# Graph network layer 3 on one core: a second DMA queue for the row sums, and two moves in the order of a period

## The chip, the cores and the metric

The kernel runs on one core of one Trainium2 chip. The metric is device time in microseconds of one execution; the time of a version is the median of several executions. The engines are TensorE (PE, with its weight loads shown apart as PEld), VectorE (DVE), ScalarE (ACT), GpSimd (POOL) and SyncE (SP), whose only work here is to issue DMAs. Each engine takes its instructions in the order in which they were written for it, and semaphores hold an instruction back until what it needs is there. A DMA that an engine issues is one of the instructions in that engine's order; the transfer itself then runs on the core's 16 DMA engines.

## What is computed

The input x has 32 samples of 512 nodes with 64 features, and adj is a 512 x 512 normalised adjacency with few entries. Four layers follow one another, each with a layer norm and a ReLU in front and x added behind. The first three (a graph convolution, a two-step propagation and a one-head attention) take the first 440 us or so and are not touched. The fourth, "layer 3", is this:

```python
def gat_layer(x, graph, W, b):
    h = x @ W
    s = jnp.einsum('bnd,bmd->bnm', h, h) * graph
    s = jnp.where(s == 0.0, NEG_INF, s)
    a = jax.nn.softmax(s, axis=2)
    return jnp.einsum('bnm,bmd->bnd', a, h) + b
heads = jax.vmap(lambda W, b: gat_layer(flow_x, graph, W, b))(Wh, bh)   # 8 heads, 128 wide
...
x = jax.nn.leaky_relu(cat, negative_slope=0.01)
out = gat_layer(x, graph, W_out, b_out)
return jax.nn.leaky_relu(out, negative_slope=0.01)
```

All of it is in float32.

## The kernel before

Layer 3 works in units of two 512 x 512 attention maps. A `Heads` unit holds two heads of one sample (32 samples x 4 = 128 units), an `Out` unit the last attention of two samples (16 units), so there are 144. The two maps lie side by side: the tiles called `p_att` are 128 rows x 2 maps x 512 columns, and a unit has four of them (r = 0 to 3). A unit passes through these steps, whose names are those of the code:

- `scores(r)` (L367, PE) writes logits to a PSUM tile of the pool `ps_s`, which has two buffers; `maxima(r)` (L379, DVE) adds the mask, keeps the negated logits in `p_att` and takes each row's extreme value into `top`.
- `spread_out` and `spread_in` (L384 to L398): DVE turns `top`, SP writes it to DRAM in four small DMAs (L389) and reads it back to all partitions in one of 512 KB (L395, tile `topb`).
- `shift(r)` (L401, POOL) subtracts `topb`; `exps(r)` (L410, ACT) takes the exponential, for r = 1 and 3 into a PSUM tile `e_ps` that shares the two buffers of `ps_s`; `join(r)` (L413, DVE) adds the pair's two exponentials.
- `totals` (L431, PE) sums the columns of the two joined tiles with a matrix of ones, and ACT copies the result to `tot` (L436). `totals_out` (L443) spreads the 4 x 512 sums over 128 partitions, eight to each, with two SP DMAs of 4 KB, one for each half e, into the tile `parts`.
- `recips` (L449, L452, DVE) adds the halves and takes the reciprocal; `recips_out` (L456, SP) writes it to DRAM; `recips_in` (L463, SP, two DMAs of 128 KB), in the next period, brings it back as `recb`.
- `values(j)` (L419, PE) multiplies with the features into one PSUM tile `av` (one buffer); `normalize` (L469, DVE), again in the next period, multiplies `av` by `recb` into `o_att` and so frees `av`.
- Heads units go on with `y_pe` (L551, PE), `y_act` (L561, ACT) and `y_dve` (L569, DVE), which leave the activated head in `cat`. `product(i)` (L597, PE, eight matmul instructions) is one quarter of the multiplication by W_out for two samples; it runs in 64 of the periods. Out units go on with `back` (L641), `back_dve`, `back_pool` (L655) and `store` (L662, SP, two DMAs of 128 KB in 256-byte runs).

The order is written out by hand, for all five engines, in `period(t)` inside `planned` (L708 to L762). Each period works on several units at once: `unit(n)` is the unit that began n periods ago. Since each engine keeps the order of that list, the place of a call fixes its place in the queue of every engine that it uses. Three stretches matter here. On SP a period issues: `recb` x2, `top_row` x4, `topb`, the two output stores if there are any, `parts` x2, `rec_row`. On PE: `scores` 2 and 3, `y_pe`, `scores` 0 and 1 of the unit ahead, `totals`, `values`, `product` if there is one, and then some small preparation (`make_v`, `make_hx`, `make_g`) before the next period's `scores(2)`. On DVE: `maxima` 2 and 3, `y_dve`, `normalize`, `maxima` 0 and 1 of the unit ahead, `join(1)`, `recips`, `join(3)`. On ACT the copy to `tot` is followed at once by `exps(1)` and `exps(3)`.

The first period that does nothing but layer 3 starts at about 463 us; a period takes 10.3 to 14 us.

Of the kernel before, what the change touches and what calls it, by code (L numbers as in the profile page):

```python
# [22 lines left out]
def fast_form(  # L23
# [25 lines left out]
    nc = tc.nc  # L49
    B, N, F = x.shape  # L50
    C = N // P
# [264 lines left out]
    class Pair:  # L316
# [121 lines left out]
        def totals_out(self):  # L438

            self.parts = tiny.tile([P, 2, 8], F32, name="parts")  # L440
            rows = self.tot.rearrange("(k e r) n -> k e r n", k=2, e=2)
            for e in range(2):
                nc.sync.dma_start(  # L443
                    self.parts[:, e], rows[:, e, 0].rearrange("k (g i) -> k g i", i=8)
                )

# [219 lines left out]
    def any_zero():  # L666

        def across(src, rows, name):
            ps = ps_m.tile([P, P], F32, name=name, tag="m")
            n = src.shape[0]  # L670
            nc.tensor.transpose(ps[:rows, :n], src, ident[:n, :n])
            return ps[:rows, :n]

        own = tiny.tile([P, 1], F32, name="own")
        nc.vector.tensor_reduce(own, least, AX.X, OP.min)
        two = tiny.tile([1, 2], F32, name="two")
        nc.vector.tensor_reduce(two[:, 0:1], across(own, 1, "own_ps"), AX.X, OP.min)
        best = tiny.tile([B // 2, 2], F32, name="best")
        nc.vector.tensor_reduce(
            best,  # L680
            across(least_out, B // 2, "out_ps").rearrange("b (k f) -> b k f", k=2),
            AX.X, OP.max,
        )
        worst = tiny.tile([B // 2, 1], F32, name="worst")
        nc.vector.tensor_reduce(worst, best, AX.X, OP.min)
        nc.vector.tensor_reduce(
            two[:, 1:2], across(worst, 1, "worst_ps"), AX.X, OP.min
        )
        flag = tiny.tile([1, 1], F32, name="flag")
        nc.vector.tensor_reduce(flag, two, AX.X, OP.min)  # L690
        nc.vector.scalar_tensor_tensor(
            again, flag, 0.0, unsound, op0=OP.is_equal, op1=OP.max
        )
# [6 lines left out]
    def planned(units, products):  # L700

        class Nothing:
            def __getattr__(self, name):
                return lambda *args: None

        nothing = Nothing()

        def period(t):  # L708
            def unit(lag):
                return units[t - lag] if 0 <= t - lag < len(units) else nothing  # L710

            now, ahead = unit(0), unit(-1)
            for r in range(2, C):
                now.scores(r)
            unit(3).recips_in()
            unit(4).y_pe()
            unit(1).shift(0)
            unit(1).exps(0)
            unit(4).y_act()
            u, i = products.get(t - 1, (None, 0))  # L720
            if u and i == H // 2 - 1:
                u.keep_product()
            unit(1).shift(2)
            unit(1).exps(2)
            for r in range(2, C):
                now.maxima(r)
            now.spread_out()
            now.spread_in()
            for r in range(2):
                ahead.scores(r)  # L730
            unit(4).y_dve()
            unit(3).normalize()
            for r in range(2):
                ahead.maxima(r)
            unit(-3).features(3)
            unit(4).back()
            unit(5).back_pool()
            unit(-2).make_gs()
            unit(5).store()
            unit(2).totals()  # L740
            unit(2).totals_out()
            unit(1).shift(1)
            unit(1).exps(1)
            for j in range(C):
                unit(2).values(j)
            u, i = products.get(t, (None, 0))
            if u:
                u.product(i)
            unit(1).join(1)
            unit(1).shift(3)  # L750
            unit(1).exps(3)
            unit(2).recips()
            unit(2).recips_out()
            unit(4).back_dve()
            unit(1).join(3)
            unit(1).make_v()
            unit(-3).make_hx()
            unit(-2).make_g()
            for step in range(3):
                unit(step - 6).features(step)  # L760
            if t == len(units):
                any_zero()  # L762

        return period
# [1065 lines left out]
```

## Time and profile before

| | us |
|---|---|
| median of 3 runs (lowest, highest) | 2160.28 (2159.49, 2162.55) |
| profiled execution, its own time | 2158.13 |
| its span on the core | 2156.3 |
| PE busy over the span | 2004.3 |
| DVE busy over the span | 1787.3 |
| POOL busy over the span | 1430.5 |
| ACT busy over the span | 1224.3 |

The span is the time from the first to the last profiled instruction of the program; the rest of an execution's time (1.8 us in the profiled one) lies around it. A wait in the profile is the idle time of an engine in front of an instruction, put down to whatever released it last. "Busy" of PE is modelled and says little about how near PE is to its limit; the waits and the chain of waits, which is followed back from the last instruction, say more. Names in the profile have an output, an arrow and inputs: `parts<-tot` is the DMA of `totals_out`.

### The profile page before, as it was taken

The numbers are of one execution on the slowest core, as the hardware profiler recorded it, in microseconds if no ns is written. First come the engines' busy times: TensorE is split into PE (matmuls) and PEld (weight loads), VectorE is DVE, ScalarE is ACT, GpSimd is POOL, SyncE is SP. The second block draws the span as 40 slices with busy tenths as digits, with TensorE's granted clock in tenths as the row PEclk, the third lists the DMA queues.
The fourth block names the chain that finished last, engine by engine and source line by source line (L and its number), as shares of the span: only waits on it lengthen the run. The fifth ranks groups of instructions, "written<-read, shape, count | busy, mean of one in ns | idle before, by whom it ended". The sixth has DMA issues, their size and how long they took to land.

```text
span 2156.3 us, 32793 instructions
## 1 busy us (share of the span) xinstructions
PE 2004.3 (93%) x11038; PEld 836.9 (39%) x11038; DVE 1787.3 (83%) x4257; ACT 1224.3 (57%) x1944; POOL 1430.5 (66%) x697
## 2 busy tenths in 40 slices
PE   7999999979989999999999999999999999999895
PEld 4676776733333333333333333333333333333231
DVE  6799997668888888888888888888889888897984
ACT  3444433336565666565656666656666666665553
POOL 2000000038788888888887888888888887887895
PEclk9999999989999999999999999999999999999998
DMA  5000000002222222222222222222222222222222
GB/s 136 1 1 2 1 1 1 1 21 76 70 65 77 74 70 75 76 65 75 75 71 71 71 71 78 66 76 69 77 71 75 65 76 71 75 66 70 75 66 76
DMA packets 135777, 129.32 MB, mean 60 GB/s; under 512 B 92792, under 2 KB 98080, under 8 KB 135472
## 3 DMA queue, kind: packets, MB, share of 16 engines
q1 hardware_dynamic: 135088, 126.94, 19.9%
q8 instruction: 89, 1.46, 0.3%
q14 instruction: 88, 0.72, 0.1%
q0 software_dynamic: 512, 0.20, 0.1%
HBM read 119.48 MB, written 5.37 MB: 58 GB/s over the span
## 4 chain that ended last, share of the span: by engine, by line
PE 50%; DVE 21%; DMA 11%; POOL 6%; ACT 5%; issue 3%; SPq 3%; POOLq 0%; DVEq 0%; ACTq 0%
PE av L419 14%; DVE p_att L379 11%; PE nt_ps L876 7%; PE s_ps L367 7%; PE acc L968 6%; POOL p_att L401 5%; DMA parts<-tot 4%; PE gT_ps L597 4%; PE g_ps L533 3%; DVE cat L569 3%; DVE p_att L413 3%; DMA topb<-top_row 2%; PE tot_ps L431 2%; DMA recb<-rec_row 2%; DVE o_att L469 2%
## 5 line engine op out<-in xcount | busy, mean ns | idle before, releaser
L401 POOL TENSOR_TENSOR p_att<-p_att,topb 128x1024 f32<-128x1024 f32 x576 | 1346.1, 2369 | 285.0 <-DMA topb<-top_row 148.9
L379 DVE CUSTOM_DVE_ANT_0 p_att<-s_ps,flow_neg 128x512 f32<-128x512 f32 x1152 | 728.6, 685 | 94.4 <-PE s_ps L367 93.2
L367 PE MATMUL s_ps<-hx,g 64*128 64x512 f32 x2048 | 542.2, 618 | 62.8 <-DVE p_att L413 50.1
L410 ACT ACTIVATE e_ps<-p_att 128x1024 f32<-128x1024 f32 x288 | 295.4, 1028 | 187.6 <-DVE top L379 89.8
L410 ACT ACTIVATE p_att<-p_att 128x1024 f32<-128x1024 f32 x288 | 304.2, 1056 | 140.1 <-POOL p_att L401 139.0
L413 DVE TENSOR_TENSOR p_att<-e_ps,p_att 128x1024 f32<-128x1024 f32 x288 | 346.4, 1203 | 35.9 <-ACT e_ps L410 35.2
L367 PEld LDWEIGHTS s_ps<-hx,g 64*128 64x128 f32 x2048 | 176.3, 186 | 371.7 <-DVE top L379 141.8
L419 PE MATMUL av<-p_att,hd 128*64 128x512 f32 x1024 | 272.7, 602 | 28.8 <-DVE o_att L469 24.8
L419 PE MATMUL av<-p_att,hn 128*64 128x512 f32 x1024 | 269.3, 592 | 0.0
L1044 POOL TENSOR_TENSOR x<-x,bias_b 128x512 f32<-128x512 f32 x16 | 20.3, 1272 | 280.5 <-DVE hn L818 280.5
L561 ACT ACTIVATE cat<-y_ps,bh 128x512 f32<-128x512 f32 x256 | 161.0, 680 | 48.0 <-PE y_ps L551 47.0
L569 DVE SCALAR_TENSOR_TENSOR cat<-y_ps,bh,cat 128x512 f32<-128x512 f32 x256 | 178.4, 738 | 11.3 <-ACT cat L561 8.5
L431 PE MATMUL tot_ps<-p_att,ones 128*32 128x512 f32 x1152 | 154.3, 608 | 3.0 <-DVE cat L569 2.5
L419 PEld LDWEIGHTS av<-p_att,hd 128*64 128x64 f32 x1024 | 71.3, 136 | 208.0 <-issue 96.8
L551 PE MATMUL y_ps<-o_att,wh_sb 64*128 64x512 f32 x512 | 142.4, 604 | 0.0
L545 ACT COPY g<-g_ps 128x512 f32<-128x512 f32 x128 | 69.6, 588 | 124.0 <-PE g_ps L533 124.0
L419 PEld LDWEIGHTS av<-p_att,hn 128*64 128x64 f32 x1024 | 85.8, 137 | 133.9 <-issue 133.9
L436 ACT COPY tot<-tot_ps 128x512 f32<-128x512 f32 x144 | 84.3, 585 | 85.1 <-ACT p_att L410 45.6
L968 PE MATMUL acc<-v,s 64*128 64x65 f32 x2048 | 124.0, 280 | 0.7 <-DVE s L954 0.4
L968 PEld LDWEIGHTS acc<-v,s 64*128 64x128 f32 x2048 | 121.1, 195 | 5.9 <-DVE o L984 1.2
L597 PE MATMUL gT_ps<-cat,wo_sb 128*64 128x512 f32 x512 | 122.2, 592 | 0.0
L876 PE MATMUL nt_ps<-adj_t,hn 128*128 128x512 f32 x256 | 117.0, 600 | 0.8 <-DVE hn L840 0.8
(181 smaller groups left out, 2014.9 us busy)
## 6 DMA issues: line engine op xcount, KB each, us to landing
topb<-top_row SPq DMA_DIRECT2D x144, 512.0 KB
recb<-rec_row SPq DMA_DIRECT2D x288, 128.0 KB
top_row<-top_t SPq DMA_DIRECT2D x576, 1.0 KB
parts<-tot SPq DMA_DIRECT2D x288, 4.0 KB
out_dram<-y SPq DMA_DIRECT2D x32, 128.0 KB
x<-in_x_dram SPq DMA_DIRECT2D x3, 1024.0 KB
rec_row<-rec_flow SPq DMA_DIRECT2D x144, 4.0 KB
x<-in_x_dram SPq DMA_DIRECT2D x4, 256.0 KB
```

What stands on the lines that cost most here:

```text
L367: nc.tensor.matmul(ps[:, k], lhsT=g[halves(k), r * P : (r + 1) * P], rhs=x[halves(k), :], start=True, stop=True,)
L379: nc.vector.tensor_tensor_reduce(out=self.p[r][:, k], in0=ps[:, k], in1=flow_neg[:, r], scale=-1.0, scalar=BIG, op0=OP.add, op1=OP.min, ac ...
L401: nc.gpsimd.tensor_tensor(self.p[r], self.p[r], self.topb, OP.subtract)
L410: nc.scalar.activation(to, self.p[r], AF.Exp, scale=-1.0)
L413: nc.vector.tensor_tensor(self.p[r], self.joined, self.p[r - 1], OP.add)
L419: nc.tensor.matmul(self.av[halves(k), :], lhsT=self.v(k, j) if j % 2 else self.less_next(k, j), rhs=self.p[j][:, k], start=(j == 0), stop= ...
L431: nc.tensor.matmul(ps[q : q + 32, :], lhsT=ones, rhs=self.p[2 * e + 1][:, k], start=True, stop=True,)
L561: nc.scalar.activation(self.cat[:, k], self.y[k], AF.Identity, bias=bh01[:, h : h + 1], scale=0.01)
L569: nc.vector.scalar_tensor_tensor(self.cat[:, k], self.y[k], bh[:, h : h + 1], self.cat[:, k], op0=OP.add, op1=OP.max,)
L597: nc.tensor.matmul(self.gps[halves(k), :], lhsT=wo_sb[:, h, :], rhs=Heads.cat.pop((self.b + k, h)), start=(h == 0), stop=(h == H - 1),)
L876: nc.tensor.matmul(p, lhsT=lhs(k), rhs=adj_t[:, k, :], start=(k == 0), stop=(k == C - 1))
L968: nc.tensor.matmul(self.acc[k][:, r], lhsT=self.s[b // 2][halves(k), b % 2, r * P : (r + 1) * P], rhs=self.v[halves(k), b], start=(b == 0) ...
```

## The change

Three edits in layer 3, nothing else. The DMA of the second half (e = 1) of `totals_out` is issued by ACT instead of SP. `unit(5).store()` moves from before `totals` to after `recips_out`. `product(i)` moves from after `values` to before it.

```diff
             self.parts = tiny.tile([P, 2, 8], F32, name="parts")
             rows = self.tot.rearrange("(k e r) n -> k e r n", k=2, e=2)
-            for e in range(2):
-                nc.sync.dma_start(
+            for e, queue in enumerate((nc.sync, nc.scalar)):
+                queue.dma_start(
                     self.parts[:, e], rows[:, e, 0].rearrange("k (g i) -> k g i", i=8)
                 )
...
             unit(-2).make_gs()
-            unit(5).store()
             unit(2).totals()
             unit(2).totals_out()
             unit(1).shift(1)
             unit(1).exps(1)
-            for j in range(C):
-                unit(2).values(j)
             u, i = products.get(t, (None, 0))
             if u:
                 u.product(i)
+            for j in range(C):
+                unit(2).values(j)
             unit(1).join(1)
             unit(1).shift(3)
             unit(1).exps(3)
             unit(2).recips()
             unit(2).recips_out()
+            unit(5).store()
             unit(4).back_dve()
```

On SP a period then issues `recb` x2, `top_row` x4, `topb`, one `parts`, `rec_row`, and the stores if there are any. On ACT the copy to `tot` is followed by the other `parts` DMA, and then by `exps(1)` and `exps(3)`. DVE and POOL keep their order.

## The prediction

> **What bounds the kernel now.** I read the page first (who is busy, and the chain that ended last), then the waits of layer 3 alone (480 to 2110 us), then the instruction timeline of one ordinary period on three engines.
>
> ```profile
> PE 2004.3 (93%) x11038; PEld 836.9 (39%) x11038; DVE 1787.3 (83%) x4257; ACT 1224.3 (57%) x1944; POOL 1430.5 (66%) x697
> ...
> PE 50%; DVE 21%; DMA 11%; POOL 6%; ACT 5%; issue 3%; SPq 3%; POOLq 0%; DVEq 0%; ACTq 0%
> ```
>
> No engine is the bound by itself. PE holds half the chain, DVE a fifth, and transfers a tenth, of which the page gives the transfer `parts<-tot`, the subject of the first edit, 4% of the span: 94 us in 37 pieces by my count along that chain. Now the waits:
>
> ```profile
> DVE p_att L379 <- PE s_ps L367: 92.0, 80, 2.7
> DVE rec_flow L449 <- DMA parts<-tot: 85.6, 105, 2.6
> PE s_ps L367 <- DVE p_att L413: 44.9, 58, 2.1
> PE av L419 <- DVE o_att L469: 24.8, 74, 1.6
> PEld av L419 <- DVE o_att L469: 21.3, 20, 1.9
> ```
>
> (Total us, times, longest.) PE and DVE wait for each other by turns. I sorted these waits by whether the period has a W_out step (64 periods, mean 11.9 us) or not (the rest, mean 11.3 us). With a step PE is the bound: DVE stands 66.5 us in 56 of the 64 before its next `maxima`, for PE's scores, so that its 52 us of waiting for `parts` there cost next to nothing. Without a step DVE is the bound more often: it waits 34 us for `parts` (mean 0.45 us over the 77 such periods that have a `join` behind it), and PE stands 43 us for `join`. The last two rows are the start of `values`, which needs `av` freed by `normalize`; in idle PE time they are 11.6 us in 52 of the step periods and 19.0 us in 62 of the others.
>
> Now one period without a step (start, duration, engine):
>
> ```profile
> 1746.16 0.58 ACT L436 COPY tot<-tot_ps 128x512 f32<-128x512 f32 x1 [0.58 <-ACT p_att L410]
> 1747.46 1.03 ACT L410 ACTIVATE e_ps<-p_att 128x1024 f32<-128x1024 f32 x1 [0.71 <-DVE top L379]
> 1749.10 1.03 ACT L410 ACTIVATE e_ps<-p_att 128x1024 f32<-128x1024 f32 x1 [0.61 <-POOL p_att L401]
> ```
> ```profile
> 1746.33 0.35 SPq L395 DMA_DIRECT2D topb<-top_row  x1
> 1746.77 1.15 SPq L443 DMA_DIRECT2D parts<-tot  x2
> 1750.57 0.34 SPq L456 DMA_DIRECT2D rec_row<-rec_flow  x1
> ```
> ```profile
> 1748.52 1.23 DVE L413 TENSOR_TENSOR p_att<-e_ps,p_att 128x1024 f32<-128x1024 f32 x1
> 1750.13 0.17 DVE L449 TENSOR_REDUCE rec_flow<-parts 128x8 f32<-128x16 f32 x1 [0.39 <-DMA parts<-tot]
> 1750.34 0.20 DVE L452 RECIPROCAL rec_flow<-rec_flow 128x8 f32<-128x8 f32 x1
> 1750.46 1.17 DVE L413 TENSOR_TENSOR p_att<-e_ps,p_att 128x1024 f32<-128x1024 f32 x1
> ```
>
> Three things are to be seen. The SP issues `topb` and both `parts` without a pause, two times 0.57 us for the latter. After the copy to `tot` ends at 1746.74, ACT stands 0.71 us for DVE's `maxima(0)`, which must free a PSUM buffer before the exponential may write `e_ps`: this is the room for a DMA issue on ACT. And the `parts` wait of 0.39 us is followed by a `join(3)` whose exponential had ended at 1750.13, 0.33 us before it began: even with `parts` there at once, DVE would gain no more than that 0.33.
>
> **What the Trainium skill says.** "DMA: Bandwidth & Descriptors", section "Issuing engines are not separate DMA queues", says that issuing from several engines saves only sequencer time, since the transfers run on the same 16 engines. Its section "Queues, rings and completion order" says that SP and ACT each own a ring on each of those engines, and that an engine turns between rings packet by packet. "Why a DMA increments its semaphore by 16 and not by 1" says that a transfer whose slowest dimension is 2 on one side uses two engines; a `parts` DMA reads from two rows (k). The trace agrees where it can: at 1006 us `topb` is issued at 1006.40 and the two `parts` at 1006.80 and 1007.42; the first 64 pairs of 32-byte packets run from 1008.97 to 1009.35, the second follow at once, to 1009.73. Two completion marks end each batch. The first batch thus begins 2.2 us after its issue, where the small `top_row` DMAs need 0.76, directly behind the 4 KB packets of `topb` on its two engines. So the second issue is not what `parts` waits for: the queue behind `topb` is. "Perfetto Trace Analysis", section "DMA Instruction — HWDGE (DVE, Sync)", says that one descriptor generator is shared and locked while in use; no run so far shows two engines issuing at once.
>
> **The change, part by part.** Sums are against the profiled execution, 2158.13 us (span 2156.3 plus 1.8 around it), which lies 2.15 us under the median.
>
> *W_out steps in front of values.* Nothing is added: the same eight instructions, 1.72 us in the chain, stand before `values` instead of behind. They need `cat`, whose second half DVE writes 0.7 us after the first, while `totals`, which starts after the first half, takes 1.04 us; so I expect no new wait. Meanwhile `normalize` ends, 0.2 us or so after `totals`. The 11.6 us of idle in step periods go. `values` ends where the product ended before; its `av` is read some 4 us later. In 56 of 64 such periods PE leads and the gain passes to DVE: 11.6 x 0.87 = 10 us. Bounds: 5 (half is eaten at the next wait) and 11.6.
>
> *A `parts` DMA on ACT.* Removed: one issue of 0.57 us on SP, plus 0.05 between. Gain in landing: 0.62 us where SP is the limit; where the ring is, both batches of 0.38 us still pass the same two engines, and only what ACT's batch can slip in between `topb`'s packets is won, 0 to 0.38 us. If the issues exclude each other, even less. In no-step periods, where DVE goes on without a pause into the next `maxima`, and with the 0.33-like cap in each, my count along the trace gives 4.9 us for a landing 0.2 us earlier, 8.1 us for 0.375 and 11.6 us for 0.6; in step periods 1.2, 2.2 and 3.6. I take 3 us in all, for some 0.1 us, and keep 0 and 15 for the range.
>
> *The same issue on ACT.* ACT's time for it is not in the trace. Nearest row: SP's 0.57 us, begun 0.11 us after the copy ends (1006.69 to 1006.80), so the exponential could start 0.7 us after the copy; were SP's own issue to hold the generator first, about 1.3 us. Today it starts 0.84 us after it in the mean over 143 periods, median 0.75, under 0.7 in 67. Behind it on ACT stand `exps(1)`, `exps(3)` and copies; DVE's `join(1)` waits for the first, PE's next scores for `join`. But `join(1)` is followed by the `parts` wait, 0.45 us, and, as measured to the next `maxima`, another 0.35 us of slack (26.7 us over 77 periods). So a hold of h us costs about 77 x (h - 0.84 - 0.45 - 0.35) = 77 x (h - 1.64): nothing at 0.7 or 1.3 in the mean. For the spread of single periods I charge 1 us; bounds 0 and 27 (h = 2.0). The ACT issue also waits for the earlier `recb` transfer that shares its semaphore; `exps(1)` already waits for that through `normalize`.
>
> *Stores later.* In 16 periods two issues of 0.6 us and the 256-byte packets leave the way of `parts`; nearly all have a W_out step, where a `parts` wait is free. They go to SP between `rec_row` (0.34 us) and `recb`, which waits 1.5 us for `rec_row` to land: 1.3 us of issue fits in. Their packets delay `recb` by up to 1 us, but `rec_row` leaves 1.4 us earlier in those periods. Zero, bounds -3 and +8 (0.5 x 16).
>
> Sum: -10 - 3 + 1 + 0 = -12, 2146 profiled, 2148 as a median.
>
> **The rivals.**
> - *The landing really comes 0.6 us sooner.* For: SP's `parts` issues are 20 us of the chain (39 pieces). Against: the queue behind `topb`. -11.6 - 15 + 1 = -26: 2134. Chance 0.13.
> - *No change.* The PE time freed in step periods reappears as waiting for POOL, which is busy 1363 of 1630 us and has its own loop from `maxima` over `topb` (6 us), four shifts (9.35 us), exponential and `join` back to `maxima`, near two periods; ACT's hold eats the rest. For: POOL's shifts are 5% of the chain. Against: POOL itself waits 147 us for `topb`. -3: 2157. Chance 0.17.
> - *Slower: ACT is held.* A DMA on ACT with its waits keeps the exponentials 2.0 us behind the copy instead of 0.84, in every period: 77 x 0.36 = +27, less 10 from the product: 2177. It decides from h = 1.64 + 10/77 = 1.8 us. For: a third of the periods have under 0.65 us of room. Against: SP does the same issue in 0.57. Chance 0.18.
>
> **How the numbers follow.** Forecast 0.52, the others 0.13, 0.17, 0.18. This kernel's runs tell 0.2%, 4.3 us, from no change. Faster by that: 0.13, 0.47 of the forecast (the rest gains too little) and 0.02 of the third: 0.62. Within: 0.05 of the forecast, 0.13 of the third and 0.02 of the last: 0.20. Slower: 0.16 of the last and 0.02 of the third: 0.18. The forecast's own range is 2141 to 2156 (-19 to -4). Over all cases I leave out the slow half of the last one and the extreme of the first: 2136 to 2165.
>
> **What would show it.** Right: PE's wait for `normalize` at `values` drops to about 19 us plus weight loads' share, with none in periods with a step; DVE's wait for `parts` shrinks by a tenth of a microsecond or so in ordinary periods and vanishes in those with stores; ACT's issue lasts about 0.6 us; and `join` waits for `e_ps` (23.2 us now) grow little. Wrong: a `join` wait of 0.5 us per period, an ACT issue over 1.2 us, or a PE wait in front of the W_out steps. A `parts` wait below half of today's 85.6 us would mean the larger gain.

## The result, and the profile after

The changed kernel takes 2143.76 us in the median of five runs (2141.73 to 2145.79), the kernel before 2159.49 us beside it (2154.81 to 2162.55). The ratio is 0.9931, with a 95% interval of 0.9915 to 0.9946: 14.9 us faster (11.7 to 18.4). Its profiled execution took 2145.48 us, 12.65 less than the one of before.

The page of the kernel after, busy shares and the chain by engine and by line:

```profile
PE 1998.9 (93%) x11038; PEld 819.4 (38%) x11038; DVE 1788.2 (83%) x4257; ACT 1225.9 (57%) x1944; POOL 1431.3 (67%) x697
...
PE 48%; DVE 17%; DMA 13%; POOL 11%; issue 4%; ACT 4%; SPq 2%; POOLq 0%; ACTq 0%; DVEq 0%
POOL p_att L401 10%; PE av L419 10%; DVE p_att L379 9%; PE s_ps L367 8%; PE nt_ps L876 7%; DMA parts<-tot 6%; PE acc L968 6%; PE gT_ps L597 4%; DMA topb<-top_row 4%; DVE p_att L413 4%; PE tot_ps L431 3%; PE g_ps L533 2%; DMA top_row<-top_t 2%; SPq L389 2%; ACT e_ps L410 1%
```

The busy times of PE, DVE, ACT and POOL are within 0.3% of those of before, as they must be: nothing was taken out. The transfer `parts<-tot` has not left the chain; it has 6% now and had 4%. So the chain gives no sign that the gain comes from a shorter transfer. POOL's shifts went from 5% to 10%: in this execution the chain runs over `topb` and POOL more often.

The waits of layer 3, 480 to 2110 us, in the kernel after (total us, times, longest):

```profile
DVE p_att L379 <- PE s_ps L367: 87.3, 82, 2.1
DVE rec_flow L449 <- DMA parts<-tot: 64.2, 100, 2.1
PE s_ps L367 <- DVE p_att L413: 54.8, 61, 8.9
DVE p_att L413 <- ACT e_ps L410: 40.9, 53, 2.9
PE av L419 <- DVE o_att L469: 14.2, 42, 1.9
PEld av L419 <- DVE o_att L469: 14.1, 11, 2.8
```

Two of these answer to the edits. PE's wait for `normalize` at `values`, 24.8 and 21.3 us before, is down to 14.2 and 14.1. Sorted by period, the 11.6 us of PE idle in the 64 periods with a W_out step are gone altogether; 17.1 us stay in the others (19.0 before). And DVE waits 21.4 us less for `parts` (85.6 before), but 17.7 us more for the exponential in front of `join`. Its row in the kernel before:

```profile
DVE p_att L413 <- ACT e_ps L410: 23.2, 39, 1.2
```

Together these two are 108.8 us before and 105.1 after: DVE waits there almost as long as before. In part one wait stands in for the other, as the experiments will show. In part the stores have left the way: in the ten or eleven periods of this stretch that have them, the wait for `parts` fell from 16.1 to 4.5 us.

The third row, PE's wait for `join`, only looks longer than before (44.9 us). Every kernel has one such wait of some 8.9 us at the start of layer 3, at 476.68 us before and 478.88 us after, and only the later one reaches into the stretch that begins at 480 us. Without it 45.9 us are left.

### The profile page after: what moved, and what is told of

Read it like the earlier page. It is cut to its first block, busy times and chain, and to the rows that moved or that the text cites. A ratio compares the mean times of both kernels' runs of the same rounds, so it can differ in the third digit from the quotient of the medians.

```text
span 2143.7 us, 32958 instructions
## 1 busy us (share of the span) xinstructions
PE 1998.9 (93%) x11038; PEld 819.4 (38%) x11038; DVE 1788.2 (83%) x4257; ACT 1225.9 (57%) x1944; POOL 1431.3 (67%) x697
## 4 chain that ended last, share of the span: by engine, by line
PE 48%; DVE 17%; DMA 13%; POOL 11%; issue 4%; ACT 4%; SPq 2%; POOLq 0%; ACTq 0%; DVEq 0%
POOL p_att L401 10%; PE av L419 10%; DVE p_att L379 9%; PE s_ps L367 8%; PE nt_ps L876 7%; DMA parts<-tot 6%; PE acc L968 6%; PE gT_ps L597 4%; DMA topb<-top_row 4%; DVE p_att L413 4%; PE tot_ps L431 3%; PE g_ps L533 2%; DMA top_row<-top_t 2%; SPq L389 2%; ACT e_ps L410 1%
## 5 line engine op out<-in xcount | busy, mean ns | idle before, releaser
L569 DVE SCALAR_TENSOR_TENSOR cat<-y_ps,bh,cat 128x512 f32<-128x512 f32 x256 | 178.3, 738 | 12.8 <-ACT cat L561 10.5
L419 PEld LDWEIGHTS av<-p_att,hn 128*64 128x64 f32 x1024 | 80.0, 137 | 139.8 <-issue 139.8
```

The costliest lines, as they stand in the source:

```text
L419: nc.tensor.matmul(self.av[halves(k), :], lhsT=self.v(k, j) if j % 2 else self.less_next(k, j), rhs=self.p[j][:, k], start=(j == 0), stop= ...
L569: nc.vector.scalar_tensor_tensor(self.cat[:, k], self.y[k], bh[:, h : h + 1], self.cat[:, k], op0=OP.add, op1=OP.max,)
```

## The experiments

All ratios are to the kernel before, run on the same chip beside each of them, with 95% intervals. 2157 us is taken as the time of before where a ratio is turned into microseconds.

**One edit at a time.** Theory A: the moved W_out steps carry the gain. Theory B: the second DMA queue does. Theory C: the stores do. The first three kernels make one edit of the change each, and the fourth makes all but the ACT edit.

```diff
# moved steps alone
-            for j in range(C):
-                unit(2).values(j)
             u, i = products.get(t, (None, 0))
             if u:
                 u.product(i)
+            for j in range(C):
+                unit(2).values(j)
```

> The W_out steps in front of values alone. Theory A (the moved steps carry the gain): the PE idle at the start of values in the 64 periods with a step, 11.6 us, goes to zero and the time falls by 10 to 13 us, ratio 0.994 to 0.9955. Theory B (the second DMA queue carries it): less than half of the 15 us, ratio above 0.9965. Theory C (the stores carry it): the same, above 0.9965.

Measured: 0.9941 (0.9927 to 0.9954), -12.7 us. No PE idle is left at `values` in step periods. Counted from `totals` to the next `totals`, a period with a step takes 11.77 us in the mean instead of 12.00, one without a step 11.15 instead of 11.17: the gain lies where the edit acts. The row of the wait, 24.8 us in the kernel before:

```profile
PE av L419 <- DVE o_att L469: 15.7, 45, 1.7
```

```diff
# ACT edit alone
-            for e in range(2):
-                nc.sync.dma_start(
+            for e, queue in enumerate((nc.sync, nc.scalar)):
+                queue.dma_start(
```

> One parts DMA on ACT alone. Theory A: the ring behind topb sets the landing, so the last parts packet stays at 3.4 us after the issue of topb and the time moves by less than 3 us, ratio 0.9985 to 1.0015. Theory B (the second queue carries the gain): -6 us or more, ratio under 0.997, and DVE's wait for parts falls by 0.3 us a period, 40 us in all. A hold of ACT that costs more than it brings would give a ratio above 1.002.

Measured: 0.9992 (0.9981 to 1.0004), -1.7 us, not to be told from nothing. The last `parts` packet passes 3.39 us after the issue of `topb` (median over the periods, from the packets of the trace); in the kernel before it was 3.41.

```diff
# stores alone
-            unit(5).store()
             unit(2).totals()
...
             unit(2).recips_out()
+            unit(5).store()
```

> The stores after rec_row alone. Theory A: the parts wait shrinks by about 1 us in each of some 9 periods with stores and a W_out step, where DVE would wait for PE anyway: time within 2 us, ratio 0.999 to 1.001. Theory C (the stores carry the gain): -5 us or more, ratio under 0.998. A late recb behind the store's packets would give up to +8 us, ratio 1.004.

Measured: 1.0011 (1.0000 to 1.0022), +2.4 us, at the edge of what can be told. DVE's wait for `parts` fell from 85.6 to 73.1 us for it, almost all of it in the periods with stores (16.1 to 4.8 us), and the time did not follow.

The change without the ACT edit:

> The whole change without the ACT edit. Theory A: within 3 us of the whole change, ratio 0.993 to 0.9955. Theory B: the gain is mostly gone, ratio above 0.9965. If the ACT edit costs more than it brings, this is below the whole change, under 0.992.

Measured: 0.9939 (0.9924 to 0.9953), against 0.9931 (0.9915 to 0.9946) for the whole. Theory A holds, and B and C fall: the moved steps are the change, and the other two edits are worth nothing that these runs can tell.

**How much has to stand in front of `values`?** If the steps fill a wait of 0.2 us, half a step is enough.

```diff
-        def product(self, i):
+        def product(self, i, hs=(0, 1)):
...
-            for h in range(2 * i, 2 * i + 2):
+            for h in (2 * i + a for a in hs):
...
+                u.product(i, (0,))
             for j in range(C):
                 unit(2).values(j)
...
-                u.product(i)
+                u.product(i, (1,))
```

> Only one half of each W_out step (0.86 us) in front of values, the other half behind, nothing else. Theory A (the steps fill PE's wait for normalize, 0.2 us in most periods): nearly all of the gain, ratio 0.9935 to 0.996, idle at values in step periods under 1.5 us. Rival (the gain comes from values being followed directly by the next scores, or from freeing cat sooner): half of the gain, ratio 0.9965 to 0.998.

Measured: 0.9930 (0.9909 to 0.9950), and no idle at `values` in step periods. Half a step does as much as a whole one. It is the wait that is filled, and the place behind `values` is not what hurt.

**Why the second queue brings nothing.** In the kernel after, the two batches of packets can be told apart by their rings. The batch from SP's ring starts 2.95 us after the issue of `topb` and ends at 3.40; the one from ACT's ring starts at 2.60 and ends at 3.02 (medians). ACT's issue comes at 0.3 us or so, and its packets have a ring of their own, but they start exactly where the first batch started before, 2.60 us. The trace does not name the engine of a packet; that this is the moment when the two engines that serve them are through with `topb` is inferred from the completion marks of `topb`: in 120 of 142 periods the batch begins within 0.03 us of one. With nothing in its way it could have begun far sooner. In nine periods ACT's issue came 0.74 us or more ahead of that of `topb`, and there the first packet follows the issue after 1.14 to 1.16 us. The page's queues show the second ring:

```profile
q1 hardware_dynamic: 116368, 126.35, 19.2%
q10 hardware_dynamic: 18720, 0.59, 0.5%
```

To press this further, both `parts` DMAs go to ACT, with the other two edits kept.

```diff
             for e in range(2):
-                nc.sync.dma_start(
+                nc.scalar.dma_start(
                     self.parts[:, e], rows[:, e, 0].rearrange("k (g i) -> k g i", i=8)
```

> Moved steps and later stores as in the change, but both parts DMAs on ACT, none on SP (compare with moved steps and stores without the ACT edit, ratio 0.9939). Theory A (a parts batch is served only when its two DMA engines are through with topb, whichever ring it stands in): the last parts packet stays at 3.4 us after the issue of topb, DVE's wait for parts stays within 10 us of 75, and the exponential after the tot copy starts no sooner than 1.2 us after it; the slack behind it hides that, time within 3 us, ratio 0.9925 to 0.9955. Theory B (the engines turn between the rings, and SP's ring was what held the batches): last packet 0.5 us earlier or more, wait under 45 us, ratio at or under 0.992. A hold that costs: ratio above 0.9955.

Measured: 0.9964 (0.9946 to 0.9982). The packets did what theory A says: start at 2.58 us, last one at 3.38, though none of them stands in SP's ring. Neither theory had the rest right; the ratio is where the third case, a hold that costs, had put it. The waits of the kernel without the ACT edit (total us, times, longest):

```profile
DVE rec_flow L449 <- DMA parts<-tot: 75.3, 105, 2.1
PE s_ps L367 <- DVE p_att L413: 44.6, 60, 1.6
DVE p_att L413 <- ACT e_ps L410: 30.2, 48, 2.7
PE tot_ps L431 <- DVE cat L569: 2.3, 6, 0.5
```

The same waits of this kernel:

```profile
DVE p_att L413 <- ACT e_ps L410: 89.7, 128, 6.4
PE s_ps L367 <- DVE p_att L413: 51.4, 63, 8.9
DVE rec_flow L449 <- DMA parts<-tot: 11.9, 24, 0.9
PE tot_ps L431 <- DVE cat L569: 6.2, 11, 1.3
```

The wait for `parts` is nearly gone from the list, 75.3 to 11.9 us, without the transfer landing any sooner. DVE waits in front of `join(1)` instead, 30.2 to 89.7 us, because ACT issues two DMAs before the exponential: it starts 1.29 us after the copy to `tot` in the mean (never under 1.19), where it starts 0.76 us after it in the kernel before. The rows with the longest waits of 6.4 and 8.9 us hold the start of layer 3, which this run has inside the stretch and the other has not; without these two waits 83.3 us are left in front of `join(1)`, and PE's wait for `join` is 42.5 us, no more than before. So the wait for `parts` lost 63 us and its neighbour took 53, and for the 10 us between them nothing was gained: by the difference of the ratios this kernel is 5 us slower than the one without the ACT edit. The two intervals, 0.9946 to 0.9982 and 0.9924 to 0.9953, overlap a little, so that the 5 us are at the edge of what can be told. Where they arise is not shown. One way that hangs on ACT, and not on `parts`, is that of `cat`: DVE waits 12.1 us instead of 8.6 for ACT's part of it, and PE 6.2 us instead of 2.3 for `cat` in front of `totals`, which takes a PSUM buffer that `cat` frees.

**Are the sums or the row extremes the tighter way?** Here `topb` is issued behind SP's `parts` DMA, in the whole change.

```diff
             now.spread_out()
-            now.spread_in()
...
             unit(2).totals_out()
+            now.spread_in()
```

> The whole change, with SP's topb issue put behind its parts issue. Theory A: with topb no longer ahead, the parts packets start 0.8 us after their issue and DVE's wait for parts falls under 15 us; topb is issued some 0.6 to 1 us later, so POOL's wait for topb grows, by 30 us or more. The parts wait is worth at most 12 us; which of the two wins tells whether the way over topb and POOL is the tighter one: ratio to before 0.987 if not, 0.995 to 1.005 if so. Theory B (the batches do not wait for topb but for the two engines' own small packets): the parts wait stays above 40 us.

Measured: 1.0220 (1.0198 to 1.0243), 62 us more than the whole change. Waits of this kernel (total us, times, longest):

```profile
POOL p_att L401 <- DMA topb<-top_row: 201.8, 92, 4.5
DVE p_att L413 <- ACT e_ps L410: 76.0, 118, 2.8
DVE cat L569 <- ACT cat L561: 74.5, 90, 1.4
PE tot_ps L431 <- DVE cat L569: 56.7, 75, 1.2
DVE rec_flow L449 <- DMA parts<-tot: 2.4, 5, 0.7
```

And the chain, by engine and by line:

```profile
PE 41%; POOL 20%; DMA 13%; ACT 10%; DVE 9%; issue 4%; SPq 2%; POOLq 0%; ACTq 0%; DVEq 0%
POOL p_att L401 19%; DMA topb<-top_row 12%; PE nt_ps L876 7%; PE av L419 6%; PE s_ps L367 6%; PE acc L968 5%; PE tot_ps L431 5%; DVE p_att L379 3%; PE gT_ps L597 3%; ACT p_att L410 3%; DVE p_att L413 2%; ACT e_ps L410 2%; PE g_ps L533 2%; DVE cat L569 2%; ACT tot L436 2%
```

With `topb` out of their way the last `parts` packet passes 1.95 us after the first `parts` issue, 3.09 in the kernel after (medians over 141 periods, from the packets of the trace). So it is `topb` that they stand behind. Their wait drops to 2.4 us, and the kernel is much slower: 62 us over 144 periods is 0.43 us a period. I had put the worst at a ratio of 1.005, for a `topb` issued 0.6 to 1 us later. It is issued 1.6 us later, since SP now waits for the copy to `tot` first (3.99 us after `top` is turned, 2.35 in the kernel after, medians), so that part of the miss is a larger delay than I had meant. The two rows with `cat` show how a late `topb` reaches PE, which I had overlooked. On ACT `exps(0)`, which needs `shift(0)` and so `topb`, stands ahead of `y_act`. So ACT's part of `cat` comes late (DVE waits 74.5 us for it, 10.5 in the kernel after), `y_ps` holds its two PSUM buffers longer, and `totals`, which needs one of them, waits 56.7 us instead of 3.9. The row extremes are the tighter way.

**Can other periods be filled in the same way?** The transposes of `make_hx` and the matmuls of `make_g` stand behind `values` and need nothing from it.

```diff
             if u:
                 u.product(i)
+            elif t >= 0 and not isinstance(unit(1), Out):
+                unit(-3).hx_pe()
+                unit(-2).g_pe()
             for j in range(C):
                 unit(2).values(j)
```

> The moved W_out steps, and in periods without such a step the matmuls of make_hx and make_g put in front of values too (no new work, evacuations where they were; periods with make_v left as they are). Theory A (any PE work that needs nothing new hides the wait for normalize): the 17 us of idle at values in periods without a step fall below 6, and the time falls by 3 to 8 us more than with the moved steps alone (ratio 0.9941), to 0.990 to 0.993. Rival (those periods are DVE's, so that the PE time reappears before the scores): idle at values falls alike, ratio 0.993 to 0.995.

Measured: 1.0025 (1.0010 to 1.0041), 18 us above the moved steps alone. The idle at `values` in periods without a step fell to 7.3 us as both had it, but PE's time in `make_g` rose. Only the first matmul of `make_g` was moved next, which does not need the PSUM buffer that `tot` still holds.

```diff
-                unit(-2).g_pe()
+                unit(-2).g_pe(0)
```

> As the fill run, but in periods without a W_out step only the transposes of make_hx and the first of the two matmuls of make_g stand in front of values, so that no PSUM buffer is needed that tot still holds. Theory A (what made the fill run slow was PE waiting for tot's PSUM buffer in front of values): that loss of some 20 us is gone, ratio 0.991 to 0.9945. Rival (the preparation in front of values costs by itself, since values, and all that follow them, end later): still slower than the moved steps alone, ratio above 0.996.

Measured: 1.0001 (0.9987 to 1.0015), 13 us above the moved steps alone; theory A's reason is not enough, and the number is that of the rival. What the rival leaves open is why preparation in front of `values` should cost anything. The `make_g` row in the groups of PE's instructions, in the kernel before (busy time, mean ns of one):

```profile
L533 PE MATMUL g_ps<-hx,m 64*128 64x512 f32 x256 | 83.1, 648 | 6.8 <-ACT g L545 6.1 <-ACT hx L300 0.7
```

In the first fill:

```profile
L546 PE MATMUL g_ps<-hx,m 64*128 64x512 f32 x256 | 101.8, 648 | 6.8 <-ACT g L565 6.1 <-ACT hx L534 0.7
```

In the second:

```profile
L548 PE MATMUL g_ps<-hx,m 64*128 64x512 f32 x256 | 107.7, 648 | 6.7 <-ACT g L567 6.1 <-ACT hx L535 0.7
```

The same 256 instructions, each as long as before, fill 18.7 us and 24.6 us more of PE. They are pairs: each uses half of TensorE's rows (the 64 of 64*128), and the two run side by side when they follow each other directly. Of the 64 pairs, 55 run side by side in the kernel before, 32 in the first fill and 33 in the second. What parts 23 of them in the first is the PSUM buffer, held until ACT has copied `tot`; in the second `values` stands between the two halves of 22 pairs. PE then does one after the other. That is as much as the fills fell behind the moved steps alone, 18 and 13 us, or more. A fill that keeps all pairs together was not run, so it is not shown that this is the whole of it.

**Spreading the W_out steps.** Step periods are PE's (DVE waits for scores there), the others are more often DVE's. So the load was made even: first by giving each sample its own step in its own period, in front of `values` and then behind it.

```diff
-            for h in range(2 * i, 2 * i + 2):
-                for k in range(2):
-                    nc.tensor.matmul(
+            for h in range(2 * i, 2 * i + 2):
+                nc.tensor.matmul(
...
-            if b % 2:
-                products[len(flow) + 3] = out_unit, i
+            products[len(flow) + 3] = out_unit, i, b % 2
```

> W_out steps in front of values, and spread evenly: each Heads unit multiplies its own two heads in its own period (0.86 us in 128 periods, instead of 1.72 us in 64). Same work in all. If periods with a step are PE's and those without are DVE's, the first lose 0.86 us and the second take 0.86 us into PE's idle time (0.27 us at values, 0.67 us before the scores): theory A says 20 us or more under the moved steps alone, ratio 0.980 to 0.988. Rival (the bound is the way over topb and POOL, the same in both kinds of period): within 5 us of the moved steps alone, ratio 0.992 to 0.996.

> W_out steps spread evenly as in the run before, but behind values, where the kernel before has them. Theory A (in front of values they fill the wait for normalize, some 0.2 us in each of 128 periods): 10 to 20 us above the even run in front. Rival (the place no longer counts once the load is even): within 4 us of it.

Measured: 1.0171 (1.0147 to 1.0194) in front, 1.0297 (1.0273 to 1.0321) behind. My premise of the same work in all was wrong. The row of the W_out matmuls, with the moved steps alone:

```profile
L597 PE MATMUL gT_ps<-cat,wo_sb 128*64 128x512 f32 x512 | 124.0, 605 | 0.0
```

In the even run in front:

```profile
L596 PE MATMUL gT_ps<-cat,wo_sb 128*64 128x512 f32 x512 | 247.1, 605 | 0.0
```

Again pairs, here of two samples on the two halves of TensorE's columns: in the trace of the moved steps they start 7 ns apart and a pair takes 0.43 us; alone, one takes 0.43 us. In all, PE is busy 2095.6 us in the even run in front and 2002.0 with the moved steps alone: 94 us more and not 123, which fits that the first matmuls of `values` begin beside the single W_out ones there (at 1503.94 and 1504.02 us, for one), as `values` works on both halves of the columns and one is free. So these two runs say nothing on evenness. On the place they agree with the runs above, but not cleanly: 27 us lie between them, more than the 10 to 20 expected, of which the idle time at `values` is 21.5 us (in step periods behind, none in front); and behind `values` the single matmuls have nothing beside them, PE being busy 2110.6 us.

Then with the pairs kept: one half of a step in its own period, the other four periods later. The heads' `cat` is held in single tiles, since it lives longer, and the Out units come four places later.

```diff
-                products[len(flow) + 3] = out_unit, i
+                products.setdefault(len(flow) + 3, []).append((out_unit, 2 * i))
+                products.setdefault(len(flow) + 3 + (4 if b < B - 1 else 0), []).append((out_unit, 2 * i + 1))
...
-            due.append((len(flow) + LATE, out_unit))
+            due.append((len(flow) + (10 if b < B - 1 else LATE), out_unit))
```

> W_out steps in front of values and spread more evenly with the pairs of samples kept together: one half of a step (0.86 us) in its own period, the other half four periods later, mostly in a period that has no step; cat is held in single tiles, the Out units come four places later. Both column halves of TensorE stay in use, which the even run had lost (its W_out matmuls took 244 us instead of 124). Theory A (step periods are PE's, the others have PE time to spare): ratio 0.980 to 0.990, under the moved steps alone. Rival (the other periods have no more to spare than the 0.27 us at values, since DVE waits for their scores as well): within 5 us of the moved steps alone, ratio 0.992 to 0.997.

Measured: 2113.66 us, ratio 0.9802 (0.9775 to 0.9830), 43 us faster than before and the fastest of all, 28 us ahead of the change itself. The waits of this kernel in layer 3:

```profile
DVE rec_flow L449 <- DMA parts<-tot: 84.0, 105, 3.4
DVE p_att L379 <- PE s_ps L367: 51.7, 77, 2.1
PE av L419 <- DVE o_att L469: 2.4, 9, 0.4
```

DVE waits 51.7 us for scores instead of 87.3 in the kernel after, and the wait for `normalize` is all but gone. The wait for `parts` is 84.0 us, as large as in the kernel before: a kernel 43 us faster did without touching it. How much of the gain comes from the later place of the Out units, or from `cat` in single tiles, was not tried apart.

## Why the prediction was right, point by point

- *W_out steps in front of `values`, forecast -10 us (5 to 11.6).* Shown: -12.7 us alone (9.9 to 15.7), and as much with half a step. The wait went, no new one came in front of the steps, and no discount was needed: I had multiplied the 11.6 us by 0.87 for the periods in which PE does not lead, and the measured gain is at or above the whole of it. The mechanism was right and the term a little small: PE's idle at `values` fell by 13.5 us in the kernel after, 30.6 to 17.1, of which 1.9 in the periods without a step.
- *A `parts` DMA on ACT, forecast -3 us (0 to -15).* Measured with the ACT hold: -1.7 us (+0.9 to -4.1), and 0.9939 without it against 0.9931 with it. The direction of the reasoning, that the queue behind `topb` and not the second issue sets the landing, is shown by the packets and by `topb` put behind. The size was smaller still: I had allowed ACT's batch to slip in between `topb`'s packets for some 0.1 us, and in the median it did not; the last packet stayed at 3.4 us. That -1.7 us is close to the -2 of this term and the next together is no proof of either: it cannot be told from nothing. The rival with 0.6 us falls.
- *The hold of ACT, forecast +1 us.* The exponential now starts at least 0.63 us after the copy, where I had 0.7, or 1.3 if the issues excluded each other. They do not here: in 128 of 144 periods the `parts` issues of SP and ACT overlap, in 31 they begin within 0.03 us of each other (at 1190.08 us, for one), and they last 0.57 and 0.51 us (medians), as they do in the other 16. One reading was off: by the trace the exponential started 0.76 us after the copy in the mean before, not 0.84; the bound of 1.64 would be 1.56. With both DMAs on ACT the mean is 1.29 us, for which 77 x (h - 1.64) gives nothing, and the kernel was some 5 us slower. If those 5 us are real, the formula left something out; it knows `join(1)` alone, and `cat` hangs on ACT too. The slower rival, 2.0 us, is refuted in its size: in the changed kernel the mean is 0.87 us.
- *Stores later, forecast 0 (-3 to +8).* Measured +2.4 us (0 to +4.7), inside the bounds. The shorter wait for `parts`, 12.5 us in all, bought nothing, as forecast: nine of the periods with stores in the stretch have a step, where DVE waits for PE. What the small loss is, if it is one, is open.
- *The sum.* -12 us forecast, -14.9 measured. The mark set for the larger gain, a `parts` wait below half, was not reached. That wait did shrink, as forecast, but its packets land no sooner, and in periods with stores it did not vanish (4.5 us are left). The mark for a `join` wait, a little growth, was exceeded (17.7 us) without harm to the total.

## What to carry to other kernels

An engine that runs in order and waits a little at the same point of every round can be helped for nothing by moving work that is ready in front of that point; half of the piece may be enough. A wait that shrinks in the list may only have moved: here one wait lost 63 us, its neighbour took 53, and the kernel became no faster. Before a wait is called longer, look whether one event at the edge of the stretch has entered the list; here a single wait of 8.9 us did. And before matmuls are moved or parted, look whether they are halves of the array that run side by side.

## What had not been expected of the hardware

- A batch of small packets from ACT's own ring did not get between the packets of a large transfer from SP's ring on the same engines: it started at 2.60 us after the issue of `topb`, as from SP's ring, though issued at about 0.3. The Trainium skill's page "DMA: Bandwidth & Descriptors", section "Queues, rings and completion order", has an engine change rings after each packet; the medians here do not show that. Five periods of the kernel after do, in which ACT's issue came 0.2 to 0.6 us ahead of that of `topb`. In the one at 1317 us, 114 of the 128 packets pass before `topb` begins; the others follow two at a time every 0.16 us, which is as long as most packets of `topb` last, until 2.42 us. Why a batch issued later gets no such turns is open.
- A DMA issue of this shape holds ACT for 0.51 us and SP for 0.57 (medians), also when both start at once.
- Two matmuls on the two column halves start 7 ns apart (W_out, with the moved steps) and take 0.43 us together; one alone takes the same 0.43 us. W_out's 512 instructions fill 124 us in pairs and 247 us alone.
